# A GRU with a residual on one core: weights loaded by chunk over all 128 rows, the first units read out gate by gate

## The chip, the cores and the metric

The kernel runs on one core of a Trainium2 chip. The metric is the device time of one execution in microseconds (us). The kernel before was run three times; its median is 1276.31 us (1276.18 to 1276.84).

## What is computed

A recurrent layer (GRU) runs over 128 time steps for 64 sequences; input, state and output are 512 wide, all in float32. Its output is added to its input. `h0` is the argument `cond_1024`.

```python
def step(h, inp):
    x_t, prop = inp
    comb = jnp.concatenate([x_t, h], axis=-1)
    z = jax.nn.sigmoid(comb @ Wz + bz)
    r = jax.nn.sigmoid(comb @ Wr + br)
    comb2 = jnp.concatenate([x_t, r * h], axis=-1)
    h_cand = jnp.tanh(comb2 @ Wh + bh)
    h_new = (1.0 - z) * h + z * h_cand
    h_next = jnp.where(prop, jnp.tanh(h_new @ Wp + bp), h_new)
    return (h_next, h_new)
...
x = x + ys        # ys: all h_new; prop holds at every fourth step but the last
```

The rows 0 to 511 of each of Wz, Wr and Wh multiply x (the input part), the rows 512 to 1023 multiply the state (the hidden part).

## The kernel before, in words

**Two halves and four quarters.** The 64 sequences are two halves (h = 0, 1) of 32. A state tile has 128 rows: four quarters q of 32 rows, where row q*32 + b holds sequence b of the half and the q-th 128 of the 512 columns. A product of a gate (`gate`, L218) is a loop over four chunks k of 128 contraction rows, in each of which two matmuls for the half write 32 rows of PSUM each; every matmul shows as two instructions in the profile. Transposes of 32x32 blocks on VectorE (`turn`, L237; `join_x`, L245) bring states and x into the form of a left operand. For that, a chunk's rows are not 128 neighbours of the weight matrix: chunk k holds rows q*128 + k*32 to q*128 + k*32 + 31 for each q.

**A step** (`half`, L782, one generator for each half). Products of r (L794), ScalarE's sigmoid, VectorE's r*h and transpose; products of z (L808); filling units (L831, below); products of the candidate with r*h (L833), tanh, the new state and its transpose; filling units. Every fourth step has one more product with Wp (L860). ScalarE puts the input part of a gate into PSUM ahead of the hidden part's products (`seed`, L376). A small loop at the end (L874) interleaves the two generators by counting columns, which fixes the order of TensorE's work once and for all; nothing is rearranged at run time, and every engine works its own list in order.

**The input part.** Steps 0 to 3 get theirs plainly (`plain`, L434: for each step, gate and chunk a unit; two steps' units for r, z and the candidate use banks q and r of PSUM for even, a and x for odd steps; `add_bias`, L414, reads out on VectorE into `cp`). From step 4 on a form with fewer products is used (`batch`, L454): it multiplies sums of weight blocks (`sum_outer`, L286; `sum_outer_1`; `sum_inner`, L296; `sum_inner_1`) with sums of x blocks on GpSimd (`sum_raw12`, `sum_raw34` and others). These units are the filling units: `put` appends them to a list, `fill` takes some from it at set places in a step (`PLACES`, `HEAD`, `TAIL`). The first 24 units, steps 0 and 1, are done before the recurrence (L622 to L635); steps 2 and 3 come within step 0, and the first sums within step 1 (factors 1 and 2), step 2 (3 and 5) and step 3 (`begin`, L651).

**Loads.** `load_w` (L98) has a transfer for each quarter: 32 rows of SBUF, some chunks k0 to k1, and on the DRAM side 32 rows for each chunk (`"(k e) n -> e k n"`). `load_x` (L91) has one for each half and quarter: 32 rows and n steps. The kernel uses the queues of SP and ACT (`both_queues`) for the start, and SP's alone afterwards. A transfer waits, on its queue, for the eighth transfer before it. The order: x of steps 0 and 1; Wr, Wz, Wh input part; from GpSimd's queue the biases and, behind a one-element copy named `held` that waits for Wr, the start state; x of steps 2 and 3; then (`later_loads`, L144) the hidden parts, x of steps 4 to 7, x of the next group of four steps (`xs`), Wp and its bias. All later x goes through `load_x` on SP: each group of four steps is loaded twice, once into `xr` for the residual and once into `xs` for the products.

**The start** (L603 to L635). TensorE multiplies zeros (`idle`) for a while, 56 matmuls in all; the biases are spread over the rows; x of steps 0 and 1 is transposed, the start state too; VectorE makes the sums of factors 1 and 2, GpSimd those of d5, 3 and 5; then the 24 plain units, the seeds, and the recurrence.

Of the kernel before, what the change touches and what calls it, by code (L numbers as in the profile page):

```python
# [18 lines left out]
def kernel(  # L19
# [68 lines left out]
    def part(q):  # L88
        return slice(q * V, (q + 1) * V)

    def load_x(tile_, t0, n, j=0, engs=(nc.sync, nc.sync)):  # L91
        for h in range(S):
            for q in (0, 2, 1, 3):
                engs[q // 2].dma_start(  # L94
                    out=tile_[part(q), j : j + n, h, :], in_=x[ts(h, V), t0 : t0 + n, ts(q, J)]
                )

    def load_w(wt, w, k0=0, k1=K, engs=(nc.sync, nc.sync)):  # L98
        for q in (0, 2, 1, 3):
            engs[q // 2].dma_start(  # L100
                out=wt[part(q), k0:k1, :],
                in_=w[q * P + k0 * V : q * P + k1 * V, :].rearrange("(k e) n -> e k n", e=V),
            )

    both_queues = (nc.sync, nc.scalar)
# [8 lines left out]
    bias_p = const.tile([P, S, J], F32, name="bias_p")  # L114
    new_xr(0)
    load_x(xr[0], 0, 2, engs=both_queues)
    for k in range(0, K, 2):
        load_w(wx[:, :, R, :], gates_in[R][:D], k, k + 2, both_queues)
    for i in (Z, H_):
        load_w(wx[:, :, i, :], gates_in[i][:D], engs=both_queues)  # L120

    for i, b in enumerate((br, bh, bz)):
        nc.gpsimd.dma_start(out=bias_row[:, i, :], in_=b.rearrange("(o n) -> o n", o=1))

    held = const.tile([1, 1], F32, name="held")
    nc.gpsimd.tensor_copy(held, wx[0:1, 1, R, 0:1])
    for h in range(S):
        nc.gpsimd.dma_start(
            out=h_init[:, h, :],
            in_=h0[ts(h, V), :].rearrange("b (q j) -> q b j", q=NQ),  # L130
        )
    load_x(xr[0], 2, 2, 2)

    dummy = const.tile([1, 1], F32, name="dummy")
    nc.scalar.activation(dummy, ones[:, 0:1], AF.Sigmoid)
# [6 lines left out]
            load_x(xs[g], g * Q4, Q4)  # L142

    def later_loads():  # L144
        for i in range(3):
            load_w(wh[i], gates_in[i][D:], engs=both_queues)
        new_xr(1)
        load_x(xr[1], Q4, Q4)
        load_xs(2)
        load_w(wp, Wp)  # L150
        for q in range(NQ):
            nc.sync.dma_start(
                out=bias_p[part(q)],
                in_=bp.rearrange("(o d c j) -> c o d j", o=1, d=2, c=2)[q % 2].broadcast_to(
                    [V, S, J]
                ),
            )
# [79 lines left out]
    def turn(dst, src):  # L237
        nc.vector.transpose(out=dst, in_=src)  # L238
# [17 lines left out]
    def outer(kb, nb, ka):  # L256
        return wx[:, kb * S + ka, :, :].rearrange("p g (q n u) -> p n q g u", q=NQ, n=C)[:, nb]
# [27 lines left out]

    def sum_outer():  # L286
        for ka in range(S):
            nc.vector.tensor_sub(tw[3][:, ka], outer(1, 1, ka), outer(0, 1, ka))
            nc.vector.tensor_add(tw[2][:, ka], tw[3][:, ka], outer(0, 0, ka))
            nc.vector.tensor_sub(tw[4][:, ka], outer(1, 0, ka), tw[2][:, ka])  # L290

    def sum_outer_1(eng):
        for ka in range(S):
# [140 lines left out]
    def plain(t, gates=(R, Z, H_)):  # L434
        order = [(e, k) for e in gates for k in range(K)]
        if t == Q4 - 1:
            order = [(e, k) for k in range(K) for e in gates]
        return [
            plain_unit(
                t, e, k, k == 0, *((lambda: add_bias(t, gates), gates) if (e, k) == order[-1] else ())  # L440
            )
            for e, k in order
        ]
# [156 lines left out]
        T - 5: (0, 4, 3), T - 4: (0, 5, 0), T - 3: (0, 4, 0), T - 2: (0, 4, 0), T - 1: (0, 0, 0),  # L600
    }

    idle(40)  # L603
    spread(scratch[3], slice(0, 2), (R, H_))
    spread(scratch[1], slice(2, 3), (Z,))
    join_x(0, 0)
    idle(8)
    join_x(0, 1)
    idle(8)
    nc.gpsimd.tensor_sub(bias_d, bias_x[:, 1], bias0)  # L610
    later_loads()
    hT = new_T("hT", "hT_init")
    for h in range(S):
        turn(hT[:, h, :], h_init[:, h, :])
    for i in (1, 2):
        sum_inner(i, nc.vector)
        sum_inner_1(i, nc.vector)
    sum_outer_1(nc.gpsimd)
    for i in (3, 5):
        sum_inner(i, nc.gpsimd)  # L620
        sum_inner_1(i, nc.gpsimd)
    put(sum(map(list, zip(*(plain(t)[:4] for t in range(2)))), []))  # L622
    put(sum((plain(t)[n : n + 4] for n in (4, 8) for t in range(2)), []))

    def both(n):
        for _ in range(n):
            for h in range(S):
                for _ in fill(1, h):
                    pass

    both(20)
    for i in range(3):
        for h in range(1 if i == Z else S):
            seed(i, 0, h)
    both(4)  # L635

    state = {0: (h_init, hT)}
    made = {}
# [35 lines left out]

    def behind_r(t, duo, u):
        odd = FIRST + 2 * duo + 1
        if t == 1:
            sum_inner(7, nc.gpsimd)
            sum_inner_1(7, nc.gpsimd)
        if t == 2:  # L680
            pair_left(0, 1, 2)
        elif t == 3:
            pair_right(0, 1, 10)
        if t == 4:
            sum_inner(4, nc.gpsimd)
            sum_inner_1(4, nc.gpsimd)
        if u == 0 and duo >= 1 and odd - 2 < LAST:
            outer_u2(odd - 2)

    def join(t, duo, u, n):  # L690
        even, odd = FIRST + 2 * duo, FIRST + 2 * duo + 1
        if t == 0:
            join_x(0, 2 + n)
        elif t == 1:
            join_x(1, 2 + n)
        elif t == 2:
            join_x(2, n)
        elif t == 4:
            join_x(3, 2 * n)
            join_x(3, 2 * n + 1)  # L700
        elif duo >= 0 and u in (5, 6):
            join_x(even + 2, 2 * (u - 5) + n)
        elif duo >= 1 and u in (1, 3):
            join_x(odd, u - 1 + n)

    def behind_step(t, duo, u, h_new):
        g, j = divmod(t, Q4)
        even, odd = FIRST + 2 * duo, FIRST + 2 * duo + 1
        if t == T - 7:
            pair_left(0, 1, 2, LAST)  # L710
            pair_right(0, 1, 10, LAST)
        if t == 3:
            pair_left(1, 8, 9)
            pair_right(1, 8, 11)

        if duo >= 0:
            if u == 0 and duo >= 1 and odd - 2 < LAST:
                outer_c22(odd - 2)
                outer_c21(odd - 2)
            if even * Q4 < T:  # L720
                if u == 0:
                    sum_s34(even)
                elif u == 1:
                    outer_1(even)
                    outer_c11(even)
                    sum_raw12(odd)
                elif u == 2:
                    outer_u1(even)
                    outer_5(even)
                    sum_raw4(even)  # L730
                elif u == 3:
                    outer_c12(even)
                    outer_u2(even)
                    outer_c22(even)
                    if odd < LAST:
                        sum_s12(odd)
                elif u == 4:
                    if odd < LAST:
                        sum_s34(odd)
                    outer_c21(even)  # L740
                    if odd < LAST:
                        outer_1(odd)
                elif u == 5 and odd < LAST:
                    sum_raw4(odd)
                elif u == 6 and odd < LAST:
                    outer_u1(odd)
                    outer_c11(odd)
                elif u == 7 and odd < LAST:
                    outer_5(odd)
                    outer_c12(odd)  # L750
        if duo >= -1 and (even + 2) * Q4 < T:
            if t == 2 or (u == 6 and duo >= 0):
                sum_raw12(even + 2)
            if u == 7:
                sum_s12(even + 2)
        if t < T - 1:
            nc.gpsimd.tensor_add(xr[g][:, j], xr[g][:, j], h_new)  # L757

        n = 0
        if t >= T - CHUNK:  # L760
            n = 3 if t == T - 2 else 0
        elif j == Q4 - 1:
            n = 4
        if n:
            for h in range(S):
                for q in range(NQ):
                    nc.sync.dma_start(
                        out=out[ts(h, V), t - n + 1 : t + 1, ts(q, J)],
                        in_=xr[g][part(q), j - n + 1 : j + 1, h, :],
                    )  # L770
        if j == 1 and g >= 1 and (g + 1) * Q4 < T:
            new_xr(g + 1)
            load_x(xr[g + 1], (g + 1) * Q4, Q4)
        if t in (1, 2):
            load_xs(t + 2)
        if duo >= 0:
            if u == 3:
                load_xs(odd + 2)
            elif u == 6:
                load_xs(even + 4)  # L780

    def half(h):  # L782

        for t in range(T):
# [25 lines left out]
            if h == 1:  # L810
# [5 lines left out]
                join(t, duo, u, 1)  # L816
                if t == 1:
                    sum_raw34(1)
                if last:
                    nc.gpsimd.tensor_sub(xr[g][:, j], xr[g][:, j], keep)  # L820
                if t == 0:
                    sum_outer()
                    join_x(1, 0)
                    join_x(1, 1)
                    sum_raw12(1)
                    sum_inner(6, nc.gpsimd)
                    sum_inner_1(6, nc.gpsimd)
                if t == 2:
                    for n in range(2, 4):
                        join_x(2, n)  # L830
# [95 lines left out]
```

## Time and profile before

| | |
|---|---|
| median of three runs | 1276.31 us |
| the profiled execution | 1276.41 us |
| its span, first to last instruction | 1274.6 us |
| mean granted TensorE clock | 0.994 |
| bytes moved by DMA | 60.82 MB, mean 48 GB/s |
| ScalarE and GpSimd, busy share | 66% and 70% |

The profile is of one execution. Of an instruction it has the engine (PE is TensorE, PEld its weight loads, DVE VectorE, ACT ScalarE, POOL GpSimd, SP SyncE), the line in the kernel and what it writes and reads, as "out<-in" by the program's names. The page divides the span into 40 slices and gives a digit for each: tenths of the slice in which the engine was busy. A timeline lists instructions with start, duration, and in brackets how long the engine had been idle and what ended that. The queue's own issues are under SPq, ACTq and POOL. The chain of waits goes back from the last instruction to whatever released it each time. The busy times by stretches have, for each stretch, the busy us of the five engines with the number of instructions, TensorE's granted clock, the share of the 16 DMA engines that was busy, and GB/s.

### The profile page before, as it was taken

The numbers are of one execution on the slowest core, as the hardware profiler recorded it, in microseconds if no ns is written. First come the engines' busy times: TensorE is split into PE (matmuls) and PEld (weight loads), VectorE is DVE, ScalarE is ACT, GpSimd is POOL, SyncE is SP. The second block draws the span as 40 slices with busy tenths as digits, with TensorE's granted clock in tenths as the row PEclk, the third lists the DMA queues.
The fourth block names the chain that finished last, engine by engine and source line by source line (L and its number), as shares of the span: only waits on it lengthen the run. The fifth ranks groups of instructions, "written<-read, shape, count | busy, mean of one in ns | idle before, by whom it ended". The sixth has DMA issues, their size and how long they took to land.

```text
span 1274.6 us, 60714 instructions
## 1 busy us (share of the span) xinstructions
PE 1253.5 (98%) x25968; PEld 1164.3 (91%) x25968; DVE 781.5 (61%) x2161; ACT 835.6 (66%) x2685; POOL 886.8 (70%) x1027
## 2 busy tenths in 40 slices
PE   6999999999999999999999999999999999999997
PEld 3699999999999999999999999999999999999875
DVE  4656666666666666666666665666666666666544
ACT  1456667666667666666766666666666666667665
POOL 5469767787677786777687677776777777677530
PEclk8999999999999999999999999999999999999999
DMA  8302212102121111112111121111111111111010
GB/s 225 83 20 53 52 37 54 49 22 52 51 54 36 34 46 44 52 36 54 36 34 52 49 54 39 32 40 52 52 37 36 52 37 52 40 49 36 9 46 19
DMA packets 113365, 60.82 MB, mean 48 GB/s; under 512 B 12969, under 2 KB 109481, under 8 KB 113097
## 3 DMA queue, kind: packets, MB, share of 16 engines
q1 hardware_dynamic: 110628, 53.46, 16.1%
q8 instruction: 205, 3.36, 1.2%
q10 hardware_dynamic: 2212, 3.34, 0.9%
q14 instruction: 64, 0.52, 0.1%
q0 software_dynamic: 256, 0.14, 0.1%
HBM read 40.11 MB, written 16.78 MB: 45 GB/s over the span
## 4 chain that ended last, share of the span: by engine, by line
PE 95%; DMA 2%; ACT 1%; issue 1%; DVE 1%; SPq 0%; ACTq 0%; POOLq 0%; POOL 0%; DVEq 0%
PE rec L209 44%; PE rec_z L209 16%; PE scratch_r L209 13%; PE scratch_q L209 10%; PE scratch_a L209 5%; PE scratch_y L209 4%; PE scratch_x L209 4%; DMA wx<-in_L_cond_Wh_dram 1%; DMA wh<-in_L_cond_Wh_dram 1%; SPq L94 0%; DMA wx<-in_L_cond_Wr_dram 0%; DMA wh<-in_L_cond_Wr_dram 0%; ACT rec_z L235 0%; ACT c L235 0%; DMA xr<-in_x_dram 0%
## 5 line engine op out<-in xcount | busy, mean ns | idle before, releaser
L209 PE MATMUL rec<-wh,rhT 128*32 128x256 f32 x4096 | 375.3, 379 | 0.1
L209 PE MATMUL rec<-wh,hT 128*32 128x256 f32 x3072 | 281.5, 379 | 1.3 <-DVE hT L238 1.3
L209 PE MATMUL rec_z<-wh,hT 128*32 128x256 f32 x3072 | 281.5, 379 | 0.1
L209 PEld LDWEIGHTS rec<-wh,rhT 128*32 128x32 f32 x4096 | 250.4, 110 | 20.0 <-ACT scratch_r L235 0.7
L235 ACT ACTIVATE scratch_r<-rec 64x128 f32<-64x128 f32 x512 | 128.0, 250 | 131.9 <-PE rec L209 67.9
L379 ACT COPY rec<-cp 64x256 f32<-64x256 f32 x512 | 189.9, 371 | 37.2 <-DVE cp L417 17.8
L209 PEld LDWEIGHTS rec<-wh,hT 128*32 128x32 f32 x3072 | 187.0, 110 | 15.2 <-ACT c L235 3.2
L209 PEld LDWEIGHTS rec_z<-wh,hT 128*32 128x32 f32 x3072 | 193.4, 110 | 7.3 <-ACT rec_z L379 0.6
L235 ACT ACTIVATE rec_z<-rec_z 64x128 f32<-64x128 f32 x512 | 128.0, 250 | 95.9 <-PE rec_z L209 83.8
L235 ACT ACTIVATE c<-rec 64x128 f32<-64x128 f32 x512 | 139.3, 272 | 62.2 <-PE rec L209 50.8
L757 POOL TENSOR_TENSOR xr<-xr,h 128x256 f32<-128x256 f32 x127 | 93.1, 734 | 93.1 <-DVE h L847 90.3
L546 POOL TENSOR_TENSOR mb<-mb,mb 128x768 f32<-128x768 f32 x58 | 106.2, 1831 | 66.9 <-DVE mb L512 66.9
L546 POOL TENSOR_TENSOR cp<-mb,mb 128x768 f32<-128x768 f32 x76 | 139.0, 1828 | 8.1 <-DVE mb L512 4.4
L546 POOL TENSOR_TENSOR cp<-mb 128x768 f32<-128x768 f32 x46 | 84.3, 1832 | 56.9 <-ACT rec_z L379 55.5
L813 DVE SCALAR_TENSOR_TENSOR keep<-rec_z,h 128x256 f32<-128x256 f32 x96 | 40.8, 425 | 133.6 <-ACT rec_z L235 130.5
L209 PE MATMUL scratch_r<-tw,s 128*32 128x192 f32 x928 | 120.9, 326 | 0.0
L485 ACT COPY cq<-scratch_q 128x384 f32<-128x384 f32 x212 | 102.1, 482 | 19.8 <-PE scratch_q L209 18.3
L502 DVE TENSOR_TENSOR cx<-scratch_r,cx 128x384 f32<-128x384 f32 x106 | 59.1, 558 | 80.6 <-PE scratch_r L209 69.3
L209 PE MATMUL scratch_q<-tt,s 128*32 128x192 f32 x928 | 103.7, 326 | 0.0
L508 DVE TENSOR_TENSOR mb<-scratch_q,cx 128x384 f32<-128x384 f32 x106 | 59.1, 557 | 57.9 <-ACT cq L485 57.7
L799 DVE TENSOR_TENSOR rh<-scratch_r,h 128x128 f32<-128x128 f32 x192 | 56.1, 292 | 60.0 <-ACT scratch_r L235 60.0
L209 PE MATMUL rec<-wh,hpT 128*32 128x256 f32 x992 | 91.4, 379 | 0.1
(182 smaller groups left out, 3823.9 us busy)
## 6 DMA issues: line engine op xcount, KB each, us to landing
out_dram<-xr SPq DMA_DIRECT2D x249, 64.0 KB, 1.8
xr<-in_x_dram SPq DMA_DIRECT2D x248, 64.0 KB, 2.1
xs<-in_x_dram SPq DMA_DIRECT2D x240, 64.0 KB, 2.2
wp<-in_L_cond_Wp_dram SPq DMA_DIRECT2D x4, 256.0 KB, 6.2
wx<-in_L_cond_Wr_dram SPq DMA_DIRECT2D x4, 128.0 KB, 3.1
wx<-in_L_cond_Wr_dram ACTq DMA_DIRECT2D x4, 128.0 KB, 3.6
wx<-in_L_cond_Wz_dram SPq DMA_DIRECT2D x2, 256.0 KB, 7.8
wx<-in_L_cond_Wz_dram ACTq DMA_DIRECT2D x2, 256.0 KB, 8.5
```

The costliest lines, as they stand in the source:

```text
L209: nc.tensor.matmul(ps[part(2 * h + c)], lhsT=left, rhs=rhs(c), start=start, stop=True, skip_group_check=True,)
L235: nc.scalar.activation(dst[ts(d, 2 * V)], gate_ps(i, h)[ts(h, 2 * V), d, :], func)
L379: nc.scalar.copy(gate_ps(i, h)[rows].rearrange("p d (c n) -> p d c n", c=C), G[t][rows, :, :, i, :].rearrange("p c d n -> p d c n"),)
L485: nc.scalar.copy(c[:, :nm], ps[:, :nm])
L502: nc.vector.tensor_add(T2[what][:, :nm], r_ps[:, :nm], T2[what][:, :nm])
L508: nc.vector.tensor_add(blocks(1, 1), runs(q_ps[:, :nm]), runs(T2[what][:, :nm]))
L546: nc.gpsimd.tensor_add(dst, a, b)
L757: nc.gpsimd.tensor_add(xr[g][:, j], xr[g][:, j], h_new)
L799: nc.vector.tensor_mul(rh[:, h, :], r_, h_old[:, h, :])
L813: nc.vector.scalar_tensor_tensor(out=keep, in0=z, scalar=1.0, in1=h_old, op0=ALU.subtract, op1=ALU.mult)
```

## The change

Every load gets another form: a weight transfer has one chunk k and all 128 rows of SBUF (four transfers of 256 KB for each matrix part), an x transfer has one step and one half and all 128 rows (64 KB). Only Wr's input part and the first x use both queues. The hidden parts move from `later_loads` to the start of the list, r's ahead of x of steps 2 and 3. `held` waits for x in place of Wr.

The first 24 units are put gate by gate (`plain_two`), and after each gate's units come its bias additions and its seeds. The idle matmuls go from 56 to 36, all ahead of x.

The sums of weights move behind: factor 1 ahead of the candidate's first units; factor 2 (VectorE), 3 and d5 (GpSimd) behind r of step 0; 5 behind z of step 0; `sum_outer` from VectorE to GpSimd and to the end of step 0; 6 to step 1; 7 to step 3. x of steps 2 and 3 is transposed before step 0 and not in it.

```diff
     def load_x(tile_, t0, n, j=0, engs=(nc.sync, nc.sync)):
-        for h in range(S):
-            for q in (0, 2, 1, 3):
-                engs[q // 2].dma_start(
-                    out=tile_[part(q), j : j + n, h, :], in_=x[ts(h, V), t0 : t0 + n, ts(q, J)]
+        for i in range(n):
+            for h in range(S):
+                engs[h].dma_start(
+                    out=tile_[:, j + i, h, :],
+                    in_=x[ts(h, V), t0 + i, :].rearrange("b (q u) -> q b u", q=NQ),
                 )
-    def load_w(wt, w, k0=0, k1=K, engs=(nc.sync, nc.sync)):
-        for q in (0, 2, 1, 3):
-            engs[q // 2].dma_start(
-                out=wt[part(q), k0:k1, :],
-                in_=w[q * P + k0 * V : q * P + k1 * V, :].rearrange("(k e) n -> e k n", e=V),
+    def load_w(wt, w, engs=(nc.sync, nc.sync)):
+        for k in range(K):
+            engs[k % 2].dma_start(
+                out=wt[:, k, :], in_=w.rearrange("(q k e) n -> k q e n", q=NQ, k=K)[k]
             )
...
     load_x(xr[0], 0, 2, engs=both_queues)
-    for k in range(0, K, 2):
-        load_w(wx[:, :, R, :], gates_in[R][:D], k, k + 2, both_queues)
+    load_w(wx[:, :, R, :], gates_in[R][:D], engs=both_queues)
     for i in (Z, H_):
-        load_w(wx[:, :, i, :], gates_in[i][:D], engs=both_queues)
+        load_w(wx[:, :, i, :], gates_in[i][:D])
+    load_w(wh[R], gates_in[R][D:])
+    load_x(xr[0], 2, 2, 2)
+    for i in (Z, H_):
+        load_w(wh[i], gates_in[i][D:])
...
-    nc.gpsimd.tensor_copy(held, wx[0:1, 1, R, 0:1])
+    nc.gpsimd.tensor_copy(held, xr[0][0:1, 1, 1, 0:1])
...
-    load_x(xr[0], 2, 2, 2)
...
     def later_loads():
-        for i in range(3):
-            load_w(wh[i], gates_in[i][D:], engs=both_queues)
...
-            nc.vector.tensor_sub(tw[3][:, ka], outer(1, 1, ka), outer(0, 1, ka))
-            nc.vector.tensor_add(tw[2][:, ka], tw[3][:, ka], outer(0, 0, ka))
-            nc.vector.tensor_sub(tw[4][:, ka], outer(1, 0, ka), tw[2][:, ka])
+            nc.gpsimd.tensor_sub(tw[3][:, ka], outer(1, 1, ka), outer(0, 1, ka))
+            nc.gpsimd.tensor_add(tw[2][:, ka], tw[3][:, ka], outer(0, 0, ka))
+            nc.gpsimd.tensor_sub(tw[4][:, ka], outer(1, 0, ka), tw[2][:, ka])
...
+    def plain_two(i):
+        put(sum(map(list, zip(*(plain(t, (i,)) for t in range(2)))), []))
+        both(2 * K)
+
+    idle(36)
+    join_x(0, 0)
+    join_x(0, 1)
+    plain_two(R)
+    spread(scratch[3], slice(0, 2), (R, H_))
+    spread(scratch[1], slice(2, 3), (Z,))
+    later_loads()
+    for t in range(2):
+        add_bias(t, (R,))
+    for h in range(S):
+        seed(R, 0, h)
+    plain_two(Z)
+    for t in range(2):
+        add_bias(t, (Z,))
+    seed(Z, 0, 0)
+    hT = new_T("hT", "hT_init")
+    for h in range(S):
+        turn(hT[:, h, :], h_init[:, h, :])
+    nc.gpsimd.tensor_sub(bias_d, bias_x[:, 1], bias0)
+    sum_inner(1, nc.vector)
+    sum_inner_1(1, nc.vector)
+    plain_two(H_)
+    for t in range(2):
+        add_bias(t, (H_,))
+    for h in range(S):
+        seed(H_, 0, h)
+    join_x(0, 2)
+    join_x(0, 3)
...
     def behind_r(t, duo, u):
-        if t == 1:
-            sum_inner(7, nc.gpsimd)
-            sum_inner_1(7, nc.gpsimd)
...
         elif t == 3:
             pair_right(0, 1, 10)
+            sum_inner(7, nc.gpsimd)
+            sum_inner_1(7, nc.gpsimd)
...
     def join(t, duo, u, n):
-        if t == 0:
-            join_x(0, 2 + n)
+        if t == 0 and n == 0:
+            sum_inner(2, nc.vector)
+            sum_inner_1(2, nc.vector)
+            nc.gpsimd.tensor_copy(held, leftover(2)[0:1, 0, 0, 0:1])
+            sum_inner(3, nc.gpsimd)
+            sum_inner_1(3, nc.gpsimd)
+            sum_outer_1(nc.gpsimd)
...
     def behind_step(t, duo, u, h_new):
+        if t == 0:
+            sum_outer()
...
                 if t == 1:
                     sum_raw34(1)
+                    sum_inner(6, nc.gpsimd)
+                    sum_inner_1(6, nc.gpsimd)
...
                 if t == 0:
-                    sum_outer()
                     join_x(1, 0)
                     join_x(1, 1)
                     sum_raw12(1)
-                    sum_inner(6, nc.gpsimd)
-                    sum_inner_1(6, nc.gpsimd)
+                    sum_inner(5, nc.gpsimd)
+                    sum_inner_1(5, nc.gpsimd)
```

More of the change, by code (lines that the diff above doesn't have):

```diff
@@ L439, in plain @@
             plain_unit(
-                t, e, k, k == 0, *((lambda: add_bias(t, gates), gates) if (e, k) == order[-1] else ())
+                t,
+                e,
+                k,
+                k == 0,
+                *((lambda: add_bias(t, gates), gates) if t > 1 and (e, k) == order[-1] else ()),
             )
@@ L601 @@
     }
[L603 to L623, printed above, removed]
     def both(n):
@@ L629, in both @@
                     pass
[L631 to L635, printed above, removed]
+    def plain_two(i):
[29 more added lines that the diff above has]
+    join_x(0, 3)
     state = {0: (h_init, hT)}
```

## The prediction

> **What bounds the kernel now.** I read the page first, then the busy time by stretches, then TensorE's timeline of the start.
>
> ```profile
> span 1274.6 us, 60714 instructions
> PE 1253.5 (98%) x25968; PEld 1164.3 (91%) x25968; DVE 781.5 (61%) x2161; ACT 835.6 (66%) x2685; POOL 886.8 (70%) x1027
> ```
>
> ```profile
> 0.00:16.59 16.59, 9.94 (x137) 4.36 (x138) 1.67 (x5) 2.41 (x5) 4.46 (x12) 0.94 0.80 213
> 16.59:31.28 14.69, 9.42 (x128) 5.23 (x129) 12.73 (x14) 1.44 (x5) 12.65 (x9) 0.73 0.91 239
> 31.28:42.87 11.59, 10.65 (x152) 5.63 (x156) 4.62 (x11) 3.09 (x11) 1.00 (x2) 0.84 0.76 176
> 42.87:1274.60 1231.73, 1223.51 (x25556) 1149.05 (x25548) 762.53 (x2133) 828.70 (x2665) 868.73 (x1005) 1.00 0.16 42
> ```
>
> The columns are length, then busy us (instructions) of PE, PEld, DVE, ACT and POOL, then PE's granted clock, DMA share, GB/s. From 42.87 us on TensorE is busy 1223.5 of 1231.7 us at full clock: that part is a block that nothing in this diff makes shorter. All that the diff can win or lose is when the block starts, and holes that it makes in the block's first steps. So I look at what the start waits for.
>
> ```profile
> 16.59 3.64 PE L209 MATMUL scratch_q<-wx,xT 128*32 128x256 f32 x32 [5.30 <-DMA xr<-in_x_dram]
> 31.28 3.64 PE L209 MATMUL rec<-wh,hT_init 128*32 128x256 f32 x28 [5.27 <-ACT rec L379]
> 42.87 0.39 PE L209 MATMUL rec<-wh,rhT 128*32 128x256 f32 x2
> ```
>
> ```profile
> 18.29 0.56 DVE L297 TENSOR_TENSOR tt<-wx 128x384 f32<-128x384 f32 x1 [3.07 <-DMA xr<-in_x_dram]
> 29.32 0.74 DVE L417 TENSOR_TENSOR cp<-scratch_q,bias_x 128x256 f32<-128x256 f32 x2
> 30.98 0.41 DVE L417 TENSOR_TENSOR cp<-scratch_x,bias_x 128x256 f32<-128x256 f32 x1
> ```
>
> ```profile
> 9.13 8.93 DMA wx<-in_L_cond_Wh_dram
> 23.75 8.34 DMA wh<-in_L_cond_Wh_dram
> ```
>
> Two waits of 5.3 us stand on TensorE. The first is for transfers. The second is for VectorE: it sums weights from 18.29 to 29.32 us, only then adds the biases (29.32 to 31.4), and ScalarE's seeds come behind that. Under both lies the chain's own load time: the candidate's hidden-state weights land at about 32 us (23.75 + 8.34), 10 us before their first use at 42.87.
>
> **The change, part by part.** The largest part is the shape of every load. Before, a weight transfer fills 32 rows and its DRAM side begins with those 32 rows. After, it fills 128 rows and its DRAM side is "q e n", so that it begins with a dimension of **four**; the x loads become "q b u", also four outermost. No load on the SP or ACT queue of before has that form, but its two last stores (L842, "q b n") have.
>
> ```profile
> 1270.17 0.68 SPq L842 DMA_DIRECT2D out_dram<-xr  x1
> 1270.95 1.15 ACTq L842 DMA_DIRECT2D out_dram<-xr  x1
> ```
>
> ```profile
> 1271.40:1272.40 1.00, 0.00 (x0) 0.00 (x0) 0.00 (x0) 0.00 (x0) 0.00 (x0) 1.00 0.24 69
> 1272.20:1273.20 1.00, 0.00 (x0) 0.00 (x0) 0.00 (x0) 0.00 (x0) 0.00 (x0) 1.00 0.26 76
> 1271.40:1273.20 1.80, 0.00 (x0) 0.00 (x0) 0.00 (x0) 0.00 (x0) 0.00 (x0) 1.00 0.25 72
> ```
>
> Nothing else runs there. Two stores of 64 KB take 1.8 us, 0.9 us each, one after the other, and the share of the 16 DMA engines is 0.25 throughout: four engines, full, and twelve idle. The loads and other stores, with 32 rows outermost, fill far more:
>
> ```profile
> 1.50:2.00 0.50, 0.50 (x8) 0.16 (x4) 0.00 (x0) 0.00 (x0) 0.50 (x2) 1.00 0.23 69
> 24.00:25.00 1.00, 1.00 (x28) 0.60 (x23) 1.00 (x2) 0.00 (x0) 1.00 (x1) 1.00 1.06 389
> 25.00:26.00 1.00, 1.00 (x20) 0.36 (x12) 0.90 (x2) 0.00 (x0) 0.92 (x2) 1.00 1.10 408
> ```
>
> So I take it that each new load works on four engines, and on the same four each time: SP's one queue carries all but four of the transfers of the start, and no row shows another four taking over. (Whether each could take its own four no row can tell; that would be the sixteen-engine rival below.) From both sides: at best such a load still fills 16 engines at 408 GB/s, at worst it has a quarter of the 239 GB/s of the busy stretch, 60 GB/s. I take a quarter of the 389 GB/s of 24:25, **97 GB/s** for 2 KB rows, and the stores' 72 GB/s for the 512-byte rows of x, since four engines alone don't press on each other as sixteen do.
>
> The Trainium skill, page "DMA: Bandwidth & Descriptors", section "Why a DMA increments its semaphore by 16 and not by 1", says that a hardware queue uses the largest number of engines up to 16 that divides the slowest dimension of both sides; by that it is four here, and the stores' 0.25 agrees. The same page's "Rules for kernel authors" recommends 128 partitions for bandwidth, which speaks for this change; by that alone the sixteen-engine rival below would be the outcome.
>
> The sum needs two more rows, for what shares the engines:
>
> ```profile
> q8 instruction: 205, 3.36, 1.2%
> ```
>
> ```profile
> h_init<-in_cond_dram POOLq DMA_DIRECT2D x2, 64.0 KB, 8.0
> ```
>
> Ahead of the candidate's last hidden-state chunk the new order puts 8 transfers of x (64 KB) and 24 of weights (256 KB). x: 65.5 KB / 72 = 0.91 us, x8 = 7.3 us. Weights: 262 KB / 97 = 2.70 us, x24 = 64.8 us. First bytes flow about 1.6 us in (the row 1.50:2.00). That is 73.7; code (3.36 MB per 1275 us) and the start state share the engines (0.3 MB in that time over 16 engines, under 1 us), and landing takes some tenths: **75 us**. Of the candidate's gate, three of four chunks can be multiplied before; in the profile of before its fourth is reached at about 44.0 us (42.87, and twelve of a half's sixteen instructions at 0.1 us). The block is shifted by 75 - 44 = **31 us**.
>
> What costs nothing under this, and why, beside three rows of TensorE and SP:
>
> ```profile
> 8.01 0.64 PE L209 MATMUL scratch_a<-wx,xT 128*32 128x256 f32 x8
> ...
> 49.78 0.39 PE L209 MATMUL rec<-wh,hT 128*32 128x256 f32 x2
> ...
> 83.52 0.40 PE L209 MATMUL rec<-wp,hT 128*32 128x256 f32 x2
> ```
>
> ```profile
> 0.76 1.81 SPq L94 DMA_DIRECT2D xr<-in_x_dram  x4
> ```
>
> The 20 idle matmuls left out, the gates read out one by one, the biases added ahead of VectorE's sums (the 5.27 us wait goes), the transposes of x steps 2 and 3 moved ahead, the earlier start state, and the ten weight issues taken off ACT's queue (SP now has 28 issues of 0.45 us, 13 us in all) all end long before 75 us: the loads hide them. If loads were quick, they would be worth about what the sixteen-engine rival says. What is late next: SP's later loads stand behind. Steps 4 and 5 of x land 1.8 and 3.6 us after 75; VectorE transposes them ahead of the first step's candidate product, so that is free at about 79.1, while before had 5.8 us from 44 to the next gate (49.8): free, with 1 us to spare. Then 12 transfers of x, 11 us, and four of Wp, 10.8 us: about 101 us. Its use at 83.52 moves to over 114. In the steady part 16 loads of x per four steps take 16 x 0.91 = 14.6 us of some 39 (1231.7 us for 127 steps): hidden.
>
> GpSimd is the other place. Behind the first step's z it gets, beyond what it had, sum_inner(5) and sum_outer, in front of the sums s34r for which the third step's units wait:
>
> ```profile
> 18.32 4.31 POOL L294 TENSOR_TENSOR d<-wx 128x768 f32<-128x768 f32 x2 [5.24 <-DMA xr<-in_x_dram]
> 48.95 1.01 POOL L297 TENSOR_TENSOR tt<-tw 128x384 f32<-128x384 f32 x1
> 53.06 0.73 POOL L757 TENSOR_TENSOR xr<-xr,h 128x256 f32<-128x256 f32 x1
> 57.84 0.47 POOL L310 TENSOR_TENSOR s34r<-xT 128x128 f32<-128x128 f32 x1
> 74.52 0.46 POOL L310 TENSOR_TENSOR s12r<-xT 128x128 f32<-128x128 f32 x1 [8.27 <-PE scratch_r L209]
> ```
>
> ```profile
> L546 POOL TENSOR_TENSOR mb<-mb,mb 128x768 f32<-128x768 f32 x58 | 106.2, 1831 | 66.9 <-DVE mb L512 66.9
> ```
>
> ```profile
> 64.91 0.33 PE L209 MATMUL scratch_y<-tt,s34r 128*32 128x192 f32 x1
> ```
>
> From 79: s12r 1.8, sum_inner(5) 4.1, sum_outer six of 128x768, 1.83 (L546) to 2.15 (L294) each (11 to 13), the residual 0.7, three of s34r 1.3: 98 to 100 us. Needed at 64.91 + 31 = 96 to 97. That is 1 to 4 us of waiting on TensorE, and more can follow, since GpSimd's reserve then (8.3 us before 74.52) is eaten up. Bounds 0 to 8; I take 3 us. VectorE loses the six sums of tw and is no bound.
>
> The clock: behind a wait of 5.27 us it was halved for 6.8 us.
>
> ```profile
> 28.00:34.90 6.90, 3.62 (x32) 1.72 (x36) 3.38 (x8) 1.79 (x5) 4.12 (x4) 0.51 0.84 183
> ```
>
> With matmuls arriving only as chunks land it may be half when the last one lands; that costs up to 3.4 us, nothing if the twelve filling units before it have warmed it. I take 1.5.
>
> Sum: 31 + 3 + 1.5 = 35.5 us on the profiled execution's 1276.41 us (its span is 1274.6; the median of the runs is 1276.31, 0.1 below): **1312 us**.
>
> **The rivals.** *Four engines, but slower.* The row 16.59:31.28 has 239 GB/s at a share of 0.91: 16.4 GB/s per busy engine, 66 on four. Then weights take 24 x 4.0 = 95 us, and the end moves by 30 more, 1342; halfway, 1327. For it: packets take longer in busy stretches; against: the two rows at 389 and 408. *Loads spread over sixteen engines after all* (the number of engines follows the SBUF side's 128 rows, and the stores look four wide for another reason, such as their issues of 0.68 and 1.15 us, which are as long as the transfers). This is the case on the faster side. 6.8 MB at 239 to 408 GB/s end at 18 to 30 us. TensorE needs from the first chunk, at 4 us, 192 plain, 64 gate and 96 filling instructions of 0.054 us (eight in the 0.43 us from one such group at 8.01 to the next at 8.44), 19 us, and the hand-overs between: its block starts 14 to 20 us earlier than at 44, less 3 us for GpSimd: about **1262 us** (1257 to 1268). The point from which it decides: the break-even is a last landing near 40 us, 6.8 MB in 38 us, 179 GB/s, 7.4 engines. Eight engines give no change, more gain. *GpSimd's new sums as the bound*: up to 8 us whatever the loads do; in the forecast it only widens the range, and it can't alone turn the sixteen-engine case slower. For doing nothing at all there is only that eight-engine case.
>
> **How the numbers follow.** Four engines at about 97 GB/s 0.72 (1300 to 1322); four and slower 0.12 (1322 to 1342); sixteen 0.13; eight 0.03. The range of 1300 to 1335 takes in the first and most of the second and leaves out under 2 in 10. Within 0.2%, 2.6 us, is about what a measurement of this kernel can't tell from no change. Faster 0.13, same 0.03, slower 0.84.
>
> **What would show it.**
>
> ```profile
> xr<-in_x_dram SPq DMA_DIRECT2D x248, 64.0 KB, 2.1
> ```
>
> Right: a DMA share near 0.25 and 70 to 100 GB/s from 2 to 100 us; weight chunks landing every 2.7 us, Wh's last near 75; that landing in the chain just ahead of the steps; sums of tw on POOL at about 2 us, and TensorE waiting once for s34r; x loads in the steady part landing later than the 2.1 us of before, with no wait behind them. Wrong: shares near 1 in the first 20 us, or the first candidate gate before 40 us.

## The result and the profile after

The changed kernel takes **1308.47 us** (median of four runs, 1308.38 to 1310.22), the kernel before 1276.41 us on the same chip (1276.18 to 1276.84): a ratio of 1.0254, 95% interval 1.0236 to 1.0272. The forecast was 1312.0 (1300 to 1335). The profiled execution took 1308.43 us with a span of 1306.7 us.

The busy times by stretches, four stretches of the changed kernel (columns as before: length, PE, PEld, DVE, ACT, POOL, clock, DMA share, GB/s):

```profile
10.00:20.00 10.00, 6.80 (x60) 2.43 (x64) 0.00 (x0) 0.00 (x0) 0.00 (x0) 1.00 0.29 107
40.00:50.00 10.00, 4.39 (x24) 0.90 (x24) 0.00 (x0) 0.50 (x3) 0.00 (x0) 0.52 0.27 98
62.70:67.70 5.00, 5.00 (x52) 2.37 (x48) 0.42 (x1) 1.00 (x4) 4.92 (x5) 0.50 0.28 106
67.70:75.00 7.30, 7.00 (x132) 3.79 (x128) 0.45 (x1) 1.83 (x6) 1.46 (x1) 1.00 0.29 95
```

The DMA share is a quarter and a little (code and the small loads) for the whole start, where before it was 0.76 to 0.91; the bytes move at 95 to 107 GB/s in place of 176 to 239. The other engines are not what holds the start up: VectorE and GpSimd do nothing at all from 10 to 20 us. TensorE's timeline shows the same from its side:

```profile
43.29 1.07 PE L209 MATMUL rec<-wh,hT_init 128*32 128x256 f32 x4 [1.42 <-DMA wh<-in_L_cond_Wr_dram]
45.87 1.18 PE L209 MATMUL rec<-wh,hT_init 128*32 128x256 f32 x8 [1.51 <-DMA wh<-in_L_cond_Wr_dram]
48.45 1.08 PE L209 MATMUL rec<-wh,hT_init 128*32 128x256 f32 x8 [1.40 <-DMA wh<-in_L_cond_Wr_dram]
54.20 0.64 PE L209 MATMUL rec_z<-wh,hT_init 128*32 128x256 f32 x2 [4.68 <-DMA wh<-in_L_cond_Wz_dram]
70.37 0.38 PE L209 MATMUL rec<-wh,rhT 128*32 128x256 f32 x2
72.13 0.64 PE L209 MATMUL rec<-wh,rhT 128*32 128x256 f32 x8 [0.30 <-DMA wh<-in_L_cond_Wh_dram]
```

Chunk by chunk it works 1.1 us, waits 1.4 and works again: the period of 2.58 us (43.29, 45.87, 48.45) is the time of one 256 KB transfer. The gap up to 54.20 holds the four transfers of x besides. The last chunk of the candidate's weights is used from 72.13 us; before, that place was reached at about 44.0. Where the rest of the loss comes from, the waits of TensorE in the first 150 us say (what waited, for what, us in total, times, longest; "..." marks rows left out, here and below):

```profile
PE rec_z L209 <- DMA wh<-in_L_cond_Wz_dram: 9.1, 4, 4.7
PE scratch_q L209 <- DMA wx<-in_L_cond_Wr_dram: 7.9, 3, 5.9
...
PE scratch_y L209 <- POOL s34r L312: 2.0, 1, 2.0
...
PE scratch_x L209 <- POOL s4r L312: 1.2, 1, 1.2
```

The two waits for GpSimd are new. How each becomes lost time is best read from one instruction that each step has, the candidate's tanh on ScalarE. In the kernel before, at steps 0, 2, 7 and 127:

```profile
44.82 0.55 ACT L235 ACTIVATE c<-rec 64x128 f32<-64x128 f32 x2 [4.92 <-PE rec L209]
70.11 0.55 ACT L235 ACTIVATE c<-rec 64x128 f32<-64x128 f32 x2 [1.54 <-PE rec L209]
122.83 0.55 ACT L235 ACTIVATE c<-rec 64x128 f32<-64x128 f32 x2
1268.59 1.15 ACT L235 ACTIVATE c<-rec 64x128 f32<-64x128 f32 x4
```

and in the changed one:

```profile
72.81 0.55 ACT L235 ACTIVATE c<-rec 64x128 f32<-64x128 f32 x2 [7.02 <-PE rec L209]
100.37 0.55 ACT L235 ACTIVATE c<-rec 64x128 f32<-64x128 f32 x2 [1.54 <-PE rec L209]
154.55 0.55 ACT L235 ACTIVATE c<-rec 64x128 f32<-64x128 f32 x2
1300.27 1.14 ACT L235 ACTIVATE c<-rec 64x128 f32<-64x128 f32 x4
```

The differences are 28.0, 30.3, 31.7 and 31.7 us. So the block starts **28.0** us late, loses **2.3** to s34r at step 2 and **1.4** to s4r in step 6, and runs 120 steps at exactly its old pace; 0.3 to 0.4 lie behind the last step. That is the 32.0 us between the two profiled executions. These shifts at steps 0, 2 and 7 are used below for each experiment, always against the kernel before. They come from the one profiled execution of each version, the times from all its executions; the profiled execution lies below the median by 2.9 us in e1, 1.3 in e2, 1.1 in e8 and 2.4 in e10, so that for these the shifts look that much better than the medians. For s34r GpSimd's own list, and TensorE right behind it:

```profile
91.24 1.82 POOL L290 TENSOR_TENSOR tw<-wx,tw 128x768 f32<-128x768 f32 x1
...
94.64 0.45 POOL L312 TENSOR_TENSOR s34r<-xT 128x128 f32<-128x128 f32 x1
```

```profile
95.15 0.36 PE L209 MATMUL scratch_y<-tt,s34r 128*32 128x192 f32 x2 [1.98 <-POOL s34r L312]
```

The last of sum_outer's six sums ends at 93.0; the residual and the sums s34r follow, and TensorE starts on the third of these as it is done.

### The profile page after: what moved, and what is told of

Its sections match the earlier page's. It is cut to its first block, busy times and chain, and to the rows that moved or that the text cites. A ratio compares the mean times of both kernels' runs of the same rounds, so it can differ in the third digit from the quotient of the medians.

```text
span 1306.7 us, 60733 instructions
## 1 busy us (share of the span) xinstructions
PE 1264.1 (97%) x25948; PEld 1158.6 (89%) x25948; DVE 766.3 (59%) x2155; ACT 835.1 (64%) x2685; POOL 894.7 (68%) x1034
## 4 chain that ended last, share of the span: by engine, by line
PE 85%; POOL 5%; SPq 5%; issue 3%; DMA 1%; DVE 0%; ACT 0%; ACTq 0%; POOLq 0%; DVEq 0%
PE rec L209 39%; PE rec_z L209 14%; PE scratch_r L209 12%; PE scratch_q L209 9%; PE scratch_a L209 4%; PE scratch_y L209 4%; PE scratch_x L209 3%; SPq L101 3%; SPq L94 1%; DMA xr<-in_x_dram 1%; POOL mb L555 1%; POOL cp L550 1%; POOL xr L772 0%; POOL tw L289 0%; POOL tw L290 0%
## 5 line engine op out<-in xcount | busy, mean ns | idle before, releaser
L209 PE MATMUL scratch_q<-wx,xT 128*32 128x192 f32 (+1 forms) x728 | 83.3, 365 | 10.9 <-DMA wx<-in_L_cond_Wr_dram 7.9
```

The source lines that it names most:

```text
L209: nc.tensor.matmul(ps[part(2 * h + c)], lhsT=left, rhs=rhs(c), start=start, stop=True, skip_group_check=True,)
```

## The experiments

The theory: the form of the loads alone makes the loss, since a transfer whose DRAM side begins with a dimension of four works on four DMA engines; the change's order is worth some us by itself, of which GpSimd's late sums take part back. The rivals: the order (everything through SP's queue, the hidden parts early) makes the loss; the 128 rows on the SBUF side make it; or one queue is the limit, and two would get eight engines. Each ratio is to the kernel before on the same chip.

| run | median us (runs) | before us | ratio, 95% interval | shift at step 0, 2, 7 |
|---|---|---|---|---|
| the change | 1308.47 (4) | 1276.41 | 1.0254, 1.0236 to 1.0272 | +28.0, +30.3, +31.7 |
| e1, old load forms | 1277.31 (10) | 1276.79 | 1.0001, 0.9992 to 1.0010 | -5.9, -4.1, -2.6 |
| e2, new load forms alone | 1308.78 (4) | 1276.79 | 1.0251, 1.0236 to 1.0266 | +29.7, +29.7, +29.7 |
| e3, 128 outermost | 1272.54 (5) | 1276.79 | 0.9963, 0.9949 to 0.9977 | -10.1, -5.5, -4.1 |
| e9, eight outermost | 1279.41 (10) | 1276.54 | 1.0021, 1.0012 to 1.0030 | 0.0, +0.8, +2.2 |
| e4, both queues | 1311.81 (4) | 1276.79 | 1.0279, 1.0263 to 1.0294 | +30.9, +33.8, +35.2 |
| e7, old form of x | 1307.59 (4) | 1276.54 | 1.0243, 1.0229 to 1.0257 | +27.8, +29.1, +30.5 |
| e5, sum_outer on VectorE | 1306.24 (4) | 1276.54 | 1.0232, 1.0218 to 1.0246 | +27.9, +28.0, +29.4 |
| e11, and factor 7 back | 1304.73 (5) | 1276.72 | 1.0220, 1.0206 to 1.0234 | +27.8, +27.9, +27.9 |
| e8, order alone | 1274.19 (11) | 1276.54 | 0.9983, 0.9975 to 0.9992 | -7.1, -4.0, -4.0 |
| e10, and sum_outer on GpSimd early | 1270.48 (5) | 1276.72 | 0.9950, 0.9938 to 0.9963 | -9.0, -9.0, -8.9 |

**The form of the loads or the order.** e1 is the changed kernel with both load functions of before, e2 the kernel before with both new ones.

```diff
 e1 (on the changed kernel); e2 is the reverse on the kernel before; ... marks lines left out
-                    in_=x[ts(h, V), t0 + i, :].rearrange("b (q u) -> q b u", q=NQ),
...
+                    out=tile_[part(q), j : j + n, h, :], in_=x[ts(h, V), t0 : t0 + n, ts(q, J)]
...
-                out=wt[:, k, :], in_=w.rearrange("(q k e) n -> k q e n", q=NQ, k=K)[k]
...
+                out=wt[part(q), k0:k1, :],
+                in_=w[q * P + k0 * V : q * P + k1 * V, :].rearrange("(k e) n -> e k n", e=V),
```

> The changed kernel with load_x and load_w in the form of before (32 rows of SBUF, 32 rows outermost on the DRAM side); order, queues and sums as changed. Four engines as the cause: DMA share near 1 in the first 20 us, the candidate's hidden weights land at 22 to 30 us, and the time falls below before: about 1265 us (1258 to 1270). One queue (SP) as the cause: stays near 1300, since SP still issues 28 transfers of the start. GpSimd's sums or the new order as the cause: stays above 1276.

> The kernel before with the two load functions of the changed kernel, nothing else: order, both queues and sums as before. Four engines as the cause: nearly the whole loss appears, DMA share about 0.27, hidden candidate weights land at 70 to 76 us, 1303 to 1312 us. Order, queue or sums as the cause: 1276 us, within 3 us.

From 10 to 20 us, e1 first, then e2:

```profile
10.00:20.00 10.00, 9.48 (x152) 4.97 (x148) 1.45 (x4) 1.90 (x6) 1.00 (x1) 0.92 0.97 283
```

```profile
10.00:20.00 10.00, 6.89 (x60) 2.47 (x64) 0.47 (x2) 0.00 (x0) 1.52 (x3) 0.50 0.30 109
```

e2 settles the sign: with the old order and the new forms the loss is 32.0 us, as large as the whole change's. The rival of the order is out. (e2's shift drifts on to 30.8 by the end, by about 0.01 us per step; what causes that stays open.) e1 is a miss: no loss, as expected, but no gain either, and its 1277 us lies where its expectation put the order or GpSimd's sums as the cause; only e2 shows that these don't make the loss. Its profiled execution, at 1274.42 us, starts the block only 5.9 us early. Z's hidden weights are four transfers of 32 rows that must all have landed before one chunk can be used (a wait of 2.8 us), and behind that wait the granted clock is 0.60 for 4.3 us, which is another 1.7 us of lost work:

```profile
28.40:32.70 4.30, 4.30 (x49) 2.81 (x53) 1.96 (x5) 0.88 (x3) 0.00 (x0) 0.60 1.11 250
```

It then gives 1.8 and 1.4 us back at s34r and s4r.

**Is it the leading dimension?** e3 and e9 change one term of the changed kernel's weight loads: the DRAM side of a 128-row transfer.

```diff
-                out=wt[:, k, :], in_=w.rearrange("(q k e) n -> k q e n", q=NQ, k=K)[k]
+                out=wt[:, k, :], in_=w[ts(k, P), :]                                      # e3
+                out=wt[:, k, :], in_=w.rearrange("(q k e) n -> k q e n", q=8, k=K)[k]    # e9
```

> The changed kernel, but a weight chunk is taken from 128 neighbouring rows of the matrix, so that the DRAM side begins with 128 in place of four; 128 rows of SBUF, 256 KB, queue and order are those of the changed kernel. The rows of a chunk are then others than the state's, so the products are not the layer's. x keeps its four-outermost form. Four engines because of the leading four: the weights fill all 16 engines, DMA share near 1 in the first 20 us, last hidden chunk before 30 us, about 1263 us (1257 to 1270). Transfers over 128 rows as such as the cause: share 0.27, 1308 us.

> The changed kernel, but a weight chunk's DRAM side is 8 blocks of 16 rows in place of 4 of 32; all else the same, x too. The rows of a chunk are then others than the state's, so the products are not the layer's. If the leading number sets the engines: eight, DMA share near 0.5 while weights flow, 190 to 200 GB/s, last hidden chunk at 38 to 43 us, first candidate gate near before's, 1278 to 1284 us. If any rows in blocks go to four engines: 1308. If only the leading four is singled out: 1272 us, as with 128.

The same stretch in e3, then in e9:

```profile
10.00:20.00 10.00, 9.48 (x136) 4.50 (x132) 0.93 (x3) 1.67 (x5) 1.38 (x2) 1.00 0.85 288
```

```profile
10.00:20.00 10.00, 9.48 (x128) 4.49 (x124) 0.76 (x2) 1.66 (x5) 1.00 (x1) 0.79 0.53 197
```

Bytes, rows in SBUF and number of transfers are the same in all three; the share is 0.29, 0.53 and 0.85 and the rate 107, 197 and 288 GB/s for a leading 4, 8 and 128. So the leading dimension sets the number of engines. The length of the contiguous blocks doesn't: e9's 16 rows are half of the change's 32, and it moves nearly twice as much. By the Trainium skill, page "DMA: Bandwidth & Descriptors", section "Why a DMA increments its semaphore by 16 and not by 1", the number is the largest up to 16 that divides the slowest dimensions of both sides; the three shares agree, being close to 4, 8 and 16 of 16. The "Rules for kernel authors" of the same page of the Trainium skill ask, for bandwidth, for 128 partitions and at least 1 MiB per transfer: e3, e9 and the change all have 128 partitions and 256 KB, and e3 and the change lie 36 us apart, so that rule alone doesn't decide here.

e9 came out as the forecast's eight-engine case had it: the block starts just when it did (shift 0.0), and only GpSimd's sums are lost. e3 has the right direction and missed in size. Its candidate gate:

```profile
32.81 0.39 PE L209 MATMUL rec<-wh,rhT 128*32 128x256 f32 x2
```

The last chunk of these weights had landed 4 us earlier, so it is no longer the loads that decide but TensorE's own work from its first weights on:

```profile
8.22 1.08 PE L209 MATMUL scratch_q<-wx,xT 128*32 128x256 f32 x8 [3.00 <-DMA wx<-in_L_cond_Wr_dram]
```

Then 6.0 us are lost up to step 7, so that 10.1 us of an earlier start leave 4.1. The waits for s34r (2.7 us) and s4r (1.1) are 3.8 of these. Behind the first of them TensorE is busy throughout, but at half the clock:

```profile
57.70:61.00 3.30, 3.29 (x44) 2.08 (x48) 0.00 (x0) 0.00 (x0) 3.14 (x4) 0.50 0.20 60
```

That is another 1.7 us of lost work. In the changed kernel the wait of 2.0 us for s34r has no such stretch behind it (granted clock 1.00 from 92 to 102 us).

**Do two queues get other engines?** e4 puts all the weight chunks on SP's and ACT's queues in turn.

```diff
-        load_w(wx[:, :, i, :], gates_in[i][:D])
-    load_w(wh[R], gates_in[R][D:])
+        load_w(wx[:, :, i, :], gates_in[i][:D], engs=both_queues)
+    load_w(wh[R], gates_in[R][D:], engs=both_queues)
...
-        load_w(wh[i], gates_in[i][D:])
+        load_w(wh[i], gates_in[i][D:], engs=both_queues)
```

> The changed kernel with all weight chunks alternating between SP's and ACT's queue. Four fixed engines as the cause: the same four serve both queues, share 0.27, the last hidden chunk lands at 72 us as before this edit, 1308 us within 2. If each queue had its own four or if SP's queue were the limit: share 0.5, last chunk near 38 us, 1280 us or less.

```profile
30.00:40.00 10.00, 0.00 (x0) 0.00 (x0) 0.00 (x0) 0.00 (x0) 0.00 (x0) 0.50 0.26 102
```

```profile
PE scratch_q L209 <- DVE cp L417: 31.1, 1, 31.1
```

102 GB/s at a share of 0.26: the second queue uses the same four engines, and the last chunk lands at 71.9 us (72.1 in the changed kernel). The 3 us above the expected 1308 are another matter. ACT's list holds its transfers ahead of the bias copies, and a transfer waits for the eighth before it; the copies ran at 54 us, the bias additions stood behind them, and TensorE waited 31.1 us for one of these to read its bank out.

**What do the x transfers cost?** e7 gives `load_x` alone its old form (16 engines); the weights keep four.

```diff
-                    in_=x[ts(h, V), t0 + i, :].rearrange("b (q u) -> q b u", q=NQ),
...
+                    out=tile_[part(q), j : j + n, h, :], in_=x[ts(h, V), t0 : t0 + n, ts(q, J)]
```

> The changed kernel with load_x alone in the form of before. Four engines in sequence: the eight transfers of x ahead of the candidate's last hidden chunk cost 0.83 us each on the four engines; in the old form 0.2 to 0.3: 4 to 5 us less, about 1304 us. If the weights alone make the queue and x fits in beside them: 1308 us.

It gained 0.9 us and not the 4 to 5 expected; the shift at step 0 hardly moved (27.8). SP's queue shows why, with its waits and the stretch it concerns:

```profile
36.75 11.17 SPq L94 DMA_DIRECT2D xr<-in_x_dram  x8
47.96 2.58 SPq L100 DMA_DIRECT2D wh<-in_L_cond_Wz_dram  x4
```

```profile
SPq L94 <- DMA wh<-in_L_cond_Wr_dram: 5.8, 3, 2.3
```

```profile
45.00:50.00 5.00, 2.26 (x16) 0.50 (x16) 0.67 (x2) 0.87 (x3) 0.00 (x0) 0.50 0.21 67
```

x of steps 2 and 3 is eight transfers in the old form and four in the new. Each waits for the eighth transfer before it, here a weight chunk (one lands every 2.57 us); so the first chunk of Wz is not issued before 47.96, 0.4 us after the last chunk of Wr has landed (47.6). The four engines run dry (67 GB/s), and the first chunk of Wz lands at 53.35, 5.8 us behind, as in the changed kernel (48.40 to 54.16). What these four transfers of x no longer took, the queue lost by having too little outstanding. Of the 0.8 us won before them, 0.15 are left when the last chunk lands (71.93 against 72.09).

**GpSimd's late sums.** e5 puts sum_outer back on VectorE at its place of before, e11 also puts the sums of factor 7 back behind r of step 1.

```diff
-            nc.gpsimd.tensor_sub(tw[3][:, ka], outer(1, 1, ka), outer(0, 1, ka))
+            nc.vector.tensor_sub(tw[3][:, ka], outer(1, 1, ka), outer(0, 1, ka))
...
-        if t == 0:
-            sum_outer()              # at the end of step 0
+                if t == 0:
+                    sum_outer()      # behind z of step 0
...
+        if t == 1:                   # e11 alone, and away from t == 3
+            sum_inner(7, nc.gpsimd)
+            sum_inner_1(7, nc.gpsimd)
```

> The changed kernel with sum_outer on VectorE again and at its place of before (behind z of step 0, ahead of the transposes of the next x). If the two waits for s34r and s4r (2.2 and 1.4 us of the 31.7) come from GpSimd's six new sums: both go, the first candidate gate stays at +28, and the time is about 1305 us. If they come from sum_inner(5) or the late x: they stay, 1308 us.

> The changed kernel with sum_outer on VectorE at its place of before (1306.24 us when run alone), and now the sums of factor 7 on GpSimd also back behind r of step 1. In the run without the second edit GpSimd is busy without a gap from 102.5 us until s4r at 143.3 to 144.5, for which TensorE waits 1.1 us, while it is idle for 7.7 us ahead of 102.5; factor 7's four sums (4.1 us) at 127.55 stand in that stretch. Theory A (factor 7's move to step 3 makes the wait for s4r): that wait goes, 1304.9 us (1304.6 to 1305.3), 28 us behind the kernel before, which is the loads' share alone. Rival B (another of GpSimd's sums, such as factor 5's, makes it): the wait of about 1.1 us stays and the time is 1306.2.

e5 lost the wait for s34r (step 2: 28.0 in place of 30.3) and, against the expectation, kept that for s4r. GpSimd's list in e5, then in e11, names the cause:

```profile
112.07 1.01 POOL L297 TENSOR_TENSOR tt<-tw 128x384 f32<-128x384 f32 x1
...
143.98 0.32 POOL L312 TENSOR_TENSOR s4r<-xT 128x64 f32<-128x64 f32 x1
```

```profile
114.51 1.82 POOL L555 TENSOR_TENSOR mb<-mb,bias_x 128x768 f32<-128x768 f32 x1 [2.51 <-DVE mb L516]
...
142.32 0.32 POOL L312 TENSOR_TENSOR s4r<-xT 128x64 f32<-128x64 f32 x1
```

In e5 GpSimd has no gap from 102.5 us to s4r, and factor 7's four sums (112.07 to 116.2) stand among that work. The expectation of e11 took the four at 127.55 for them; those are factor 4's, and e11 has them too, at 125.88. With factor 7 back in step 1, s4r is ready 1.7 us earlier, GpSimd even waits 2.5 us on the way, and the shift is 27.8 to 27.9 to the end. So the 3.7 us have two sources, sum_outer (2.3) and factor 7 (1.4), and what is left, 28.0 us in the medians, is the later start, for which TensorE waits for the loads.

**What the order is worth.** e8 takes e1, moves x of steps 2 and 3 behind Wz's hidden part, sum_outer to VectorE at its place of before, the sums of 3, d5 and 5 ahead of step 0 and those of 7 to step 1. e10 changes one thing in e8:

```diff
-                    sum_outer()          # VectorE, e8
                     join_x(1, 0)
                     join_x(1, 1)
                     sum_raw12(1)
+                    sum_outer()          # GpSimd, e10
```

> A version meant to be faster than both. Loads in the form of before, on SP as in the changed kernel, with x of steps 2 and 3 behind z's hidden part; first units gate by gate with biases ahead of VectorE's sums as changed; sum_outer on VectorE as before; GpSimd's sums 3, d5 and 5 ahead of step 0, sum 7 in step 1. If the changed order is worth the 10 us by which the kernel with 128 leading rows began its steps earlier, and GpSimd's late sums took back 5.9 of them: 1266 to 1271 us. If the old form's loads hold the start back: 1274 to 1277 us.

> The order alone with the load forms of before, as in the run of the order alone (1274.19 us), and one thing changed: sum_outer's six sums go from VectorE (37.35 to 43.1 us there, in front of step 0's candidate product at 44.71, for which TensorE waited 3.0 us) to GpSimd, right behind s12r in step 0. Theory A (VectorE's list was what held the gain of that run back): VectorE is free for the candidate product at about 42, the wait of 3.0 us for hT goes, GpSimd works from about 40 to 51 us, ends ahead of step 1's s34r (wanted at about 50 to 52), so the block comes 2 to 3 us earlier and the end with it: 1271.5 us (1270.5 to 1272.5), and no new wait for GpSimd. Rival B (GpSimd's list takes it back, as in the changed kernel): a wait of 1 to 3 us for s34r, s4r or mb shows on TensorE or VectorE in steps 2 to 7 and the time stays at 1273 to 1275.

e8 came out in its rival's range, "the old form's loads hold the start back"; but its start is 7.1 us early, and e10 has the same loads and is faster. What held e8 back is a new wait, here with VectorE's list ahead of it:

```profile
42.17 0.96 DVE L290 TENSOR_TENSOR tw<-wx,tw 128x768 f32<-128x768 f32 x1
...
44.71 0.28 DVE L853 TENSOR_TENSOR rec_z<-c,rec_z 128x128 f32<-128x128 f32 x1
```

```profile
45.81 0.41 PE L209 MATMUL rec<-wh,hT 128*32 128x256 f32 x2 [2.97 <-DVE hT L238]
```

sum_outer's six sums stand in front of step 0's candidate product, and TensorE waits 3.0 us for the state. In e10 that product and the next state's first use are at

```profile
37.65 0.28 DVE L853 TENSOR_TENSOR rec_z<-c,rec_z 128x128 f32<-128x128 f32 x1
```

```profile
40.82 0.39 PE L209 MATMUL rec<-wh,hT 128*32 128x256 f32 x2
```

with no wait, and none for GpSimd either, which had room for the six sums from 39.3 to 50.6 us. From the first candidate instruction to the next state's first use it takes 10.1 us in e8 (35.75 to 45.81) and 6.9 in e10 (33.91 to 40.82). e10 is 1270.48 us, **6.2 us below the kernel before**, the fastest version here.

## Why the prediction was right, point by point

- **Four engines.** Right, and the cause: e2, e3 and e9 show it, each from another side. "The same four each time" was a choice without a row; e4 shows it.
- **The loads' 31 us** were 28.0. The rate of a weight chunk was taken as 97 GB/s, 2.70 us; it was 102 GB/s, 2.57 us, which over 24 chunks is 3.1 us less. x took 0.83 us (0.91 taken), which over eight is 0.6 less. What comes besides (first bytes, code, start state, landing) was put at 2.9 us and took 3.8 (72.1 less 24 x 2.57 and 8 x 0.83). The mechanism held; the term that was off is the chunk's rate: a quarter of the 389 GB/s of the busy row is 24.3 GB/s per engine, and four engines had 25.5 each. Whether that is because four don't press on each other, as the prediction says, no run separates.
- **GpSimd's 3 us** were 3.7, but only 2.3 at the named place, s34r behind sum_outer. The other 1.4 at s4r came from the move of factor 7. The prediction allowed that "more can follow", but had no term for it: it counted what stands in front of one wait and not what the same engine is given in the steps behind it.
- **The clock's 1.5 us** were none at the step's start. The granted clock was half up to 67.7 us, but TensorE was busy without a hole from 62.7 with filling units and was at full speed when the last chunk landed at 72.1. The bound of 3.4 us was also too wide for its own row: of the 6.9 us at half clock TensorE worked only 3.62, so the row itself shows a loss of 1.8. The term is real all the same: e1 and e3, where the loads are quick, lose 1.7 us each to it.
- **The sum** was 35.5 us, and 32.0 came: 3.0 too much for the loads and 1.5 for the clock, 0.7 too little for GpSimd and 0.3 behind the last step.
- **What was to be free** was: x of steps 4 and 5, transposed at 73.7 and 75.4, stood ahead of the candidate product (76.7) and delayed nothing; Wp was issued by 84.3; from step 7 on the shift stays within 0.1 us, so the x loads of the steady part stay hidden.
- **The sixteen-engine rival** was priced 1262; e3 gave 1272.5. Two terms failed. The first weights were put at 4 us; they were used from 8.22, and the start gained 10.1 us, not 14 to 20. And behind the start 6.0 us were lost, not 3: waits of 2.7 and 1.1 us for GpSimd, and 1.7 by the halved clock behind the first, which this rival had no term for.
- **The eight-engine case** (no change) gave +2.9 us in e9, of which 2.2 are GpSimd's.
- **The order's own worth** was left to that rival. Alone it is nothing that can be measured (e1), 2.4 (e8) or 6.2 us (e10), by where the sums of weights and x of steps 2 and 3 go.

## What to carry to other kernels

Look at what the DRAM side of a transfer begins with, not at how many rows of SBUF it fills: a rearrangement that put a 4 in front was four engines here, on SP's queue and on SP's and ACT's together. When work is moved off the start of a kernel, draw up the receiving engine's whole list for the next several steps, since sums moved from step 1 to step 3 were what TensorE waited for, by way of s4r, in step 6. A transfer moved to a compute engine's queue, or a list of sums put ahead of a step's product, can be a wait for whoever stands behind it (31.1 us in e4, 3.0 in e8). A wait can cost more than its length: in e1 and e3 the clock was lower behind it.

## What the runs showed of the hardware beyond that

- The 128-row transfers scale nearly with their engines up to eight: 102 GB/s on four, 193 to 206 on eight, and then 288 on sixteen. That is not yet the most that sixteen carry in e3: from 14 to 18 us the share is 1.04 and the rate 389 GB/s, while the mean of 10 to 20 us has emptier stretches in it. In the trace a transfer of the changed kernel has five completion events, one of e9 nine and one of e1 sixteen. By the Trainium skill, page "DMA: Bandwidth & Descriptors", section "Why a DMA increments its semaphore by 16 and not by 1", the issuing side adds at once, without waiting for data, what the engines that take no part would have added; one event more than the engines in the first two cases agrees.
- VectorE's sums of two SBUF operands depend on what GpSimd does at the time. The same sum (L298, 128x384) takes 0.56 us in the changed kernel, where GpSimd is idle, and 1.25 in e8, beside GpSimd's sums. First the changed kernel, then e8:

```profile
59.53 0.56 DVE L298 TENSOR_TENSOR tt<-tt,wx 128x384 f32<-128x384 f32 x1
```

```profile
33.29 1.25 DVE L298 TENSOR_TENSOR tt<-tt,wx 128x384 f32<-128x384 f32 x1
```

It isn't the transfers: in e3 the same sum takes 0.56 us (at 21.50) with GpSimd idle and a DMA share of 1.07. GpSimd's side is smaller: its sums of factor 5 (L297 to L299) take 1.20 to 1.21 us in e10, beside VectorE's, and 1.01 in the changed kernel. Which of the two waits for the other in each case was not tried.
